# First convolution with band 8 mixed as well, squares issued ahead of casts, and the last projection one band later

## Chip, core and metric

One NeuronCore of a Trainium2 chip runs the whole program in one launch. The metric is device time in microseconds (us), the median of three runs. PE is the matrix engine (TensorE), DVE the vector engine, ACT the scalar engine, POOL GpSimd, SP the engine that here only issues DMAs.

## What is computed

The input x has shape (4, 128, 64, 64): batch, channels, rows, columns. Layer 0 is a group norm, four-head attention over all 4096 positions of an image, a projection and a residual sum. Layer 1 is the part that the change touches:

```python
residual = x
out = conv3x3_decomposed(x, lsq_quantize(w1, alpha1))
out = jax.nn.relu(batchnorm(out, gamma1, beta1))
out = conv3x3_decomposed(out, lsq_quantize(w2, alpha2))
out = batchnorm(out, gamma2, beta2)
out = jax.nn.relu(out + residual)
```

Both convolutions are 3x3 with 128 channels in and out and zero padding. All of it is float32; to keep that accuracy each convolution input is split into a high and a low part, and the products of both parts are summed in PSUM.

## The kernel before

Attention takes the first 2230 us or so and writes its result y0 to HBM. It works in 32 blocks of 512 positions; the last block's end (merge of its row sums, sums, reciprocal, weighing, projection, store) is left over and done within the first convolution.

The convolutions work in 16 bands, four for each image, of 16 rows each. A band's input tile t has 18 rows of 66 columns (a border of one on each side). The function `layer(i, prepare, start)` runs one convolution (i = 0 or 1). `BY_TWO[i]` says which bands go the mixed way:

- A **plain** band (`split_parts`, from line 594, and `conv`, line 813) casts t to a high part on ACT (L599, hi) and subtracts on DVE (L602, lo). PE then does 2 halves x 2 parts x 9 taps = 36 matmuls of 512 columns. The results' statistics are taken on DVE (L928) and the results copied to cv by ACT (L933).
- A **mixed** band (`mixed_parts`, line 570) makes sums and differences of rows first, so that two rows of output share products: DVE computes vo and vi (L580, L582, L583; "mix"), ACT casts them to uo and ui (L585), DVE subtracts to get lo and li (L589; "rest"). PE then does 4 results x 2 parts x 3 taps = 24 matmuls (`conv_by_two`, L846), the inner results from ui and li first, then the outer ones from uo and lo. From PSUM, ACT copies one inner result (L860, "copy"), DVE forms the inner sum and difference (L863, L865, "inner"), ACT writes the two outer results to a tile co (L870), and POOL adds co to cv by an accumulating DMA (L872). For the bands 13 and 14 DVE adds the outer results itself instead (L876, `outer_at_once`). The band's sum of squares is a pass of ACT over cv (L973, "square"), so it has to wait for that DMA.

Before the change bands 0, 1, 8 and 15 are plain in both convolutions, the others mixed.

The order of the work on each engine is written out by hand: each engine runs its instructions in the order in which the loop of `layer` emits them. At band m the loop emits: PE's matmuls of band m; then what the drain of band m and the preparation of band m + 2 need, that is ACT's copy, then `begin` (mix for band m + 2 on DVE and its casts on ACT), then `flush(1)` (the square of the mixed band before the last, kept in the list `behind`), then DVE's inner sums, `rest` for band m + 2, `later` (other work, and the load of band m + 3 by SP, with memsets of its border on POOL), and the outer results.

In the first convolution `first(m)` gives begin, rest and later. At band 3 its `begin` also weighs the last block's attention (L522), and its `later` holds the last block's projection (PE, L317) and store (a sum on DVE, L532, and a DMA on POOL, L533), then closes the attention's pools. The second convolution uses `second(m)`, whose `later` makes the next band's t by a ReLU on ACT (L1101) and loads the residual (L1138, SP). Eight of these residual loads also need nothing from the first convolution's results: SP issues them as soon as its queue comes to them, near the end of the first convolution.

The tiles t, hi, lo, vo, vi and co come from one ring of nine slots (`stack_tile`). PSUM has three double banks (tag s) and two single banks (tag a). A mixed band takes a double bank for the inner results, and for the outer ones either a second double bank or both single banks, alternating (`banks`); the projection and the last band (c_last) use single banks too.

```python
plain = [m for m in range(len(bandlist) - 1) if m not in BY_TWO[i]]
two = [m for m in range(len(bandlist) - 1) if m in BY_TWO[i]]
...
if (len(two) - 1 - two.index(m)) % 2:
    c = [psa.tile([P, FB], F32, name=f"c{i}_{b}_{g}{j}", tag="a") for j in "xy"]
else:
    c = pss.tile([P, 2, FB], F32, name=f"c{i}_{b}_{g}z", tag="s")
```

Of the kernel before, what the change touches and what calls it, by code (L numbers as in the profile page):

```python
# [78 lines left out]
def _fast_body(ctx, tc, x, norm_w, norm_b, qkv_wt, qkv_b, proj_wt, proj_b,  # L79
# [147 lines left out]
    def f32(t):  # L227
        return t.bitcast(F32)
# [336 lines left out]

    BY_TWO = (set(range(2, 15)) - {8}, set(range(2, 15)) - {8})

    def mixed_parts(t, name):  # L570

# [42 lines left out]
    def parts_of(i, m, t):  # L614
        b, g = bandlist[m]
        way = mixed_parts if m in BY_TWO[i] else split_parts
        mix, rest, ready[i, b, g] = way(t, f"{i}_{b}_{g}")
        return mix, rest
# [187 lines left out]
    def conv(parts, ps, j, w):  # L806
        hi, lo = parts
        r0 = j * RB
        n = 0
        for part in (hi, lo):  # L810
            for tap in range(TAPS):
                kh, kw = divmod(tap, 3)
                nc.tensor.matmul(ps.rearrange("p (r w) -> p r w", w=W), w[:, tap, :],  # L813
                                 part[:, r0 + kh : r0 + kh + RB, kw : kw + W],
                                 start=(n == 0), stop=(n == 2 * TAPS - 1))
                n += 1

    def conv_tile(i, b, g):
        return pss.tile([P, 2, FB], F32, name=f"c{i}_{b}_{g}", tag="s")
# [19 lines left out]
    def conv_by_two(parts, a, c, i):  # L839

        for m, ps, w in ((1, a[0], wmix[:, 0, :, :]), (2, a[1], wmix[:, 1, :, :]),
                         (0, c[0], wq[i][:, 0:3, :]), (3, c[1], wmix[:, 2, :, :])):
            n = 0
            for part in parts:
                for kw in range(3):
                    nc.tensor.matmul(ps.rearrange("p (r w) -> p r w", w=W), w[:, kw, :],  # L846
                                     part[m][:, :, kw : kw + W], start=(n == 0), stop=(n == 5))
                    n += 1
# [57 lines left out]
    def layer(i, prepare, start=None):  # L906


        plain = [m for m in range(len(bandlist) - 1) if m not in BY_TWO[i]]
        two = [m for m in range(len(bandlist) - 1) if m in BY_TWO[i]]  # L910
        st = mid.tile([P, 2 * len(plain), 6], F32, name=f"st{i}")
        sums = mid.tile([P, 4 * len(two)], F32, name=f"sums{i}")
        squares = mid.tile([P, len(two)], F32, name=f"squares{i}")
        shift = mid.tile([P, 2], F32, name=f"shift{i}")
        end = mid.tile([P, 18], F32, name=f"end{i}")
        n_plain, n_two = (float(len(u) * 2 * FB) for u in (plain, two))
        nc.gpsimd.memset(end[:, 0:1], n_plain)
        nc.gpsimd.memset(sums, 0.0)
        nc.gpsimd.memset(end[:, 3:4], n_two)

        behind = []

        def flush(left=0):
            while len(behind) > left:
                behind.pop(0)()

        def stats(m, j, ps):
            nc.vector.bn_stats(st[:, 2 * plain.index(m) + j, :], ps[:, j, :])  # L928

        def keep(m, j, ps):  # L930
            b, g = bandlist[m]
            c = 2 * g + j
            nc.scalar.copy(cv[b][:, c * FB : (c + 1) * FB], ps[:, j, :])  # L933

        def origin():
            mv = small.tile([P, 2], F32, name=f"first{i}", tag="mv")
            nc.vector.bn_aggr(mv, st[:, 0:2, :].rearrange("p j s -> p (j s)"))
            nc.vector.tensor_copy(shift[:, 0:1], mv[:, 0:1])
            nc.vector.tensor_scalar(shift[:, 1:2], mv[:, 0:1], -1.0, None, ALU.mult)

        def banks(m):
            b, g = bandlist[m]
            a = conv_tile(i, b, g)
# [4 lines that stand above are left out]
                c = [c[:, j, :] for j in range(2)]  # L948
            return [a[:, j, :] for j in range(2)], c

        done = start(banks, stats, keep, origin) if start else {}
        for m, (b, g) in enumerate(bandlist[:-1]):
            if m in done and m not in BY_TWO[i]:
                continue
            begin, rest, later = prepare(m)
            if m in BY_TWO[i]:
                if m in done:
                    a, c = done[m]
                else:
                    a, c = banks(m)  # L960
                    conv_by_two(ready[i, b, g], a, c, i)
                y = cv[b][:, 2 * g * FB : (2 * g + 2) * FB]
                k = two.index(m)
                copy, inner, outer, junk = rows_of_two(a, c, y, sums[:, 4 * k : 4 * k + 4], f"{i}_{m}",
                                                       m > 12)
                copy()
                begin()
                flush(1)
                inner()
                rest()  # L970
                later()
                outer()
                behind.append(lambda y=y, k=k, junk=junk: nc.scalar.activation(  # L973
                    junk, y, AF.Square, bias=shift[:, 1:2], accum_out=squares[:, k : k + 1]))
                continue
            ps = conv_tile(i, b, g)
            for j in range(2):
                conv(ready[i, b, g], ps[:, j, :], j, wq[i])
            begin()
            flush(1)  # L980
            rest()
            later()
            for j in range(2):
                stats(m, j, ps)
                keep(m, j, ps)
            if m == 0:
                origin()
        flush()
        nc.vector.bn_aggr(end[:, 1:3], st.rearrange("p j s -> p (j s)"))
        nc.vector.tensor_scalar(end[:, 2:3], end[:, 2:3], n_plain, None, ALU.mult)  # L990
        nc.vector.tensor_reduce(end[:, 4:5], sums, AX.X, ALU.add)
        nc.vector.tensor_reduce(end[:, 5:6], squares, AX.X, ALU.add)
        nc.vector.tensor_scalar(end[:, 4:5], end[:, 4:5], 1.0 / n_two, None, ALU.mult)
        off = small.tile([P, 1], F32, name=f"off{i}", tag="rs")
        nc.vector.tensor_tensor(off, end[:, 4:5], shift[:, 0:1], ALU.subtract)
        nc.vector.tensor_tensor(off, off, off, ALU.mult)
        nc.vector.scalar_tensor_tensor(end[:, 5:6], off, -n_two, end[:, 5:6], ALU.mult, ALU.add)
        b, g = bandlist[-1]
        for j in range(2):
            ps = psa.tile([P, FB], F32, name=f"c{i}_last{j}", tag="a")  # L1000
            conv(ready[i, b, g], ps, j, wq[i])
            c = 2 * g + j
            nc.vector.bn_stats(end[:, 6 + 6 * j : 12 + 6 * j], ps)
            nc.scalar.copy(cv[b][:, c * FB : (c + 1) * FB], ps)
        for f in prepare(len(bandlist) - 1):
            f()
        if i == 0:
            pools["bad"] = psa.tile([P, FB], F32, name="nbad", tag="a")
            nc.tensor.matmul(pools["bad"][0:1, 0:1], pools["big"], ones[:, 0:1], start=True, stop=True)
        keep_warm(10)  # L1010
        return batch_norm(i, end)
# [14 lines left out]
    def first(m):  # L1026
        begin = rest = nothing
        last = parts[len(blocks) - 1]
        if 2 < m < len(bandlist) - 2:
            begin, rest = parts_of(0, m + 2, raw[bandlist[m + 2]])  # L1030
        if m == 3:
            mix = begin

            def begin():
                last["weigh"]()
                mix()

        def later():
            if m == 3:
                last["project"]()  # L1040
                last["store"]()
                att.close()
                pools["low"] = ctx.enter_context(tc.tile_pool(name="low", bufs=1, reuse_waits="tile"))
                cv.extend(pools["low"].tile([P, N], F32, name=f"cv{b}") for b in (2, 3))
            if m == 5:
                nc.sync.dma_start(out=f32(wq[1]), in_=wqd)
            if m == 11:
                scales()
            if m == 14:
                count_bad()  # L1050
            if 2 < m < len(bandlist) - 3:
                load_band(*bandlist[m + 3])

        return begin, rest, later
# [571 lines left out]
```

## Time and profile before

| what | us |
|---|---|
| median of 3 runs | 2473.88 (2472.6 to 2473.94) |
| the profiled execution | 2472.39 |
| its span, first to last instruction | 2470.7 |
| PE busy | 2437.0 (99% of the span) |
| DVE busy | 2198.8 (89%) |
| ACT busy | 2179.9 (88%) |
| POOL busy | 300.1 (12%) |

The first convolution's bands stand from about 2234 to 2333 us in the span, the second's from 2337 to 2440; the output pass follows. Times in timelines are us from the span's start. A row of a timeline reads: start, duration, engine, line of the kernel, operation, what it writes <- what it reads, shape, count, and in brackets how long the engine sat idle before it and what ended that. A row of the chain reads: start, duration, engine and tile or line, count.

### The profile page before, as it was taken

What the parts mean: (1) busy time and instruction counts of PE and PEld (TensorE: products, weight loads), DVE (VectorE), ACT (ScalarE), POOL (GpSimd) and SP (SyncE); (2) the same over time, 40 slices, a digit from 0 to 9 for tenths busy, and PEclk for the clock granted to TensorE, in tenths of its full rate; (3) what the DMA queues carried; (4) which work ended last, traced back from release to release, by engine and by line L of the source; (5) the groups of instructions that cost most, each with busy time, mean ns of one, the idle gap of its engine ahead of it and who ended that gap; (6) DMA issues with size and microseconds to landing.
All of it is one profiled execution on the core that took longest, in us unless ns stands there. A gap on an engine that the chain in (4) does not pass through costs nothing.

```text
span 2470.7 us, 65042 instructions
## 1 busy us (share of the span) xinstructions
PE 2437.0 (99%) x28420; PEld 1449.8 (59%) x28420; DVE 2198.8 (89%) x1556; ACT 2179.9 (88%) x2436; POOL 300.1 (12%) x486
## 2 busy tenths in 40 slices
PE   9999999999999999999999999999999999999995
PEld 6555555555555555555555555555555555557774
DVE  6899888989998888899989888889999999999797
ACT  5999888999988899999998899999999999995687
POOL 2111111111011111111101111111010101011010
PEclk9999999999999999999999999999999999999997
DMA  6877677678776766688767676678666666778627
GB/s 197 189 187 167 174 176 176 167 192 207 167 163 168 181 161 165 144 206 200 174 155 174 172 174 155 158 190 205 147 145 142 152 138 142 161 150 163 154 52 239
DMA packets 154451, 415.67 MB, mean 168 GB/s; under 512 B 61968, under 2 KB 62736, under 8 KB 125488
## 3 DMA queue, kind: packets, MB, share of 16 engines
q0 software_dynamic: 48864, 291.93, 52.3%
q1 hardware_dynamic: 104576, 118.08, 17.6%
q8 instruction: 225, 3.69, 0.6%
q10 hardware_dynamic: 720, 1.44, 0.2%
q14 instruction: 66, 0.54, 0.1%
HBM read 107.75 MB, written 56.43 MB: 66 GB/s over the span
## 4 chain that ended last, share of the span: by engine, by line
PE 96%; DMA 1%; DVE 1%; issue 1%; ACT 0%; ACTq 0%; POOL 0%; SPq 0%; POOLq 0%; DVEq 0%
PE s L442 43%; PE acc L456 39%; PE c L846 3%; PE c L813 2%; PE l L488 1%; PE pq L317 1%; PE po L317 1%; PE pk L317 1%; PE pv L317 1%; DMA rm<-p 1%; PE c_last L813 1%; DVE res L1164 1%; PE c_3z L846 0%; PE c_2z L846 0%; DMA xh<-in_x_dram 0%
## 5 line engine op out<-in xcount | busy, mean ns | idle before, releaser
L444 ACT ACTIVATE p<-s 128x1024 f32<-128x1024 f32 x2048 | 1951.2, 1032 | 194.7 <-PE s L442 151.6
L471 DVE TENSOR_TENSOR r<-r,p 128x2048 f32<-128x2048 f32 x768 | 1758.1, 2289 | 62.9 <-ACT p L444 12.0
L442 PE MATMUL s<-q,k 64*128 64x512 f32 x8192 | 1136.8, 409 | 0.5 <-ACT p L444 0.5
L456 PE MATMUL acc<-p,v 128*32 128x256 f32 x16384 | 1025.8, 383 | 0.0
L442 PEld LDWEIGHTS s<-q,k 64*128 64x128 f32 x8192 | 715.5, 184 | 406.9 <-issue 164.2
L456 PEld LDWEIGHTS acc<-p,v 128*32 128x32 f32 x16384 | 462.7, 109 | 483.3 <-issue 247.8
L466 POOL DMA_DIRECT2D rm<-p x160 | 139.3, 871 | 774.2 <-ACT p L444 618.2
L352 DVE SCALAR_TENSOR_TENSOR kst<-pk,b,kst 128x512 fp32r<-128x512 f32 x32 | 24.0, 750 | 82.8 <-PE s L442 62.3
L469 DVE TENSOR_TENSOR r<-p,p 128x2048 f32<-128x2048 f32 x32 | 73.2, 2287 | 10.9 <-ACT p L444 10.9
L352 DVE SCALAR_TENSOR_TENSOR qst<-pq,b,qst 128x512 fp32r<-128x512 f32 x32 | 24.0, 751 | 59.0 <-PE s L442 48.0
L356 POOL DMA_DIRECT2D qd<-qst x31 | 23.1, 744 | 270.5 <-DVE qst L352 227.0
L492 POOL DMA_DIRECT2D r<-rm x32 | 27.0, 845 | 224.7 <-DMA rm<-p 72.0
L585 ACT CAST uo<-vo 128x1056 fp32r<-128x1056 f32 x24 | 25.9, 1080 | 22.0 <-DVE vo L580 21.7
L846 PE MATMUL c<-ui,wmix 128*128 128x512 f32 x144 | 42.2, 401 | 0.0
L846 PE MATMUL c<-li,wmix 128*128 128x512 f32 x144 | 42.0, 400 | 0.0
L356 POOL DMA_DIRECT2D kd<-kst x27 | 20.0, 742 | 177.0 <-DVE kst L352 168.3
L464 POOL DMA_DIRECT2D rm<-p x32 | 17.9, 559 | 172.6 <-ACT p L444 104.5
L351 ACT ACTIVATE kst<-pk,b 128x512 fp32r<-128x512 f32 x32 | 22.3, 700 | 17.9 <-PE pk L317 17.8
L488 PE MATMUL l<-r,ones 128*32 128x256 f32 x512 | 37.7, 379 | 0.0
L973 ACT ACTIVATE co<-cv,shift 128x1024 f32<-128x1024 f32 x24 | 27.5, 1148 | 10.1 <-DMA cv<-co 10.1
L533 POOL DMA_DIRECT2D y<-x x32 | 21.2, 663 | 124.9 <-DVE x L532 124.9
L317 PE MATMUL po<-av,wp 128*32 128x512 f32 x256 | 33.4, 593 | 0.4 <-DVE av L522 0.4
(270 smaller groups left out, 1213.1 us busy)
## 6 DMA issues: line engine op xcount, KB each, us to landing
rm<-p POOLq DMA_DIRECT2D x192, 1024.0 KB, 7.7
r<-rm POOLq DMA_DIRECT2D x32, 1024.0 KB, 7.6
q<-qd SPq DMA_DIRECT2D x248, 128.0 KB, 4.9
x<-in_x_dram SPq DMA_DIRECT2D x86, 256.0 KB, 5.6
k<-kd SPq DMA_DIRECT2D x124, 128.0 KB, 4.7
qd<-qst POOLq DMA_DIRECT2D x31, 512.0 KB, 4.8
kd<-kst POOLq DMA_DIRECT2D x27, 512.0 KB, 4.3
cv<-co POOLq DMA_DIRECT2D x20, 512.0 KB, 5.2
```

Of the source, the lines that this page charges most:

```text
L317: nc.tensor.matmul(out[cs, :], w[:, cs], x, start=True, stop=True)
L352: nc.vector.scalar_tensor_tensor(lo, ps[what], bias, t[:, 0, :], ALU.add, ALU.subtract)
L356: (nc.sync if start else nc.gpsimd).dma_start(out=dst[b, j].rearrange("s p n -> p s n"), in_=t)
L442: nc.tensor.matmul(s[:, i, :], k[r, half, c0 : c0 + P], q[r, half, part, :], start=(part == 0), stop=(part == 1))
L444: nc.scalar.activation(pts[step][:, 2 * half : 2 * half + 2, :], s, AF.Exp, scale=SCALE)
L456: nc.tensor.matmul(acc[n][h * D : (h + 1) * D, cs], v[:, kt % KB, h * D : (h + 1) * D], pt[:, h, cs], start=(kt == 0 and half == 0), stop= ...
L466: nc.gpsimd.dma_start(out=msum[n], in_=pt, accum_op=ALU.add)
L469: nc.vector.tensor_tensor(rsum[n], pts[step - 1], pt, ALU.add)
L471: nc.vector.tensor_tensor(rsum[n], rsum[n], pt, ALU.add)
L488: nc.tensor.matmul(t["l"][h * D : (h + 1) * D, cs], ones, r[:, h, cs], start=first, stop=end)
L813: nc.tensor.matmul(ps.rearrange("p (r w) -> p r w", w=W), w[:, tap, :], part[:, r0 + kh : r0 + kh + RB, kw : kw + W], start=(n == 0), stop ...
L846: nc.tensor.matmul(ps.rearrange("p (r w) -> p r w", w=W), w[:, kw, :], part[m][:, :, kw : kw + W], start=(n == 0), stop=(n == 5))
```

## The change

Three edits. Band 8 of the first convolution goes the mixed way too (the second convolution keeps it plain). In the branch of mixed bands, in both convolutions, `flush(1)` stands ahead of `begin()`, so that ACT's queue has the square of an earlier band ahead of the casts for band m + 2. The last attention block's projection and store, and the closing of the attention's pools, stand at band 4 of the first convolution instead of band 3.

```diff
-    BY_TWO = (set(range(2, 15)) - {8}, set(range(2, 15)) - {8})
+    BY_TWO = set(range(2, 15)), set(range(2, 15)) - {8}
...
                 copy()
+                flush(1)
                 begin()
-                flush(1)
                 inner()
                 rest()
                 later()
...
         def later():
-            if m == 3:
+            if m == 4:
                 last["project"]()
                 last["store"]()
                 att.close()
```

As a result the first convolution has 13 mixed bands instead of 12, and `two.index(m)` of bands 9 to 14 grows by one, so the alternation of PSUM banks keeps its place for bands 9 to 14 and is turned over for bands 2 to 7.

## The prediction, made before the changed kernel had run

> **What bounds the kernel now.** First the page's chain of work that ended last: it is TensorE (PE) for 96% of the span, and PE is busy for 99%. So an edit counts by what it does to PE's own work, or by making PE wait. The change touches the two convolution stages only (2234 to 2440 us), so I then asked for busy time by stretch: bands 2 to 7, plain band 8, bands 9 to 14 of the first convolution.
>
> ```profile
> core 0: us, PE busy (x) PEld busy (x) DVE busy (x) ACT busy (x) POOL busy (x), PEclk, DMA share, GB/s
> 2245.90:2281.50 35.60, 35.60 (x153) 27.16 (x152) 33.36 (x52) 25.32 (x46) 5.80 (x18) 1.00 0.98 188
> 2281.50:2290.10 8.60, 8.60 (x37) 6.78 (x37) 5.63 (x8) 3.91 (x8) 1.29 (x7) 1.00 1.18 233
> 2290.10:2324.40 34.30, 34.30 (x145) 27.08 (x144) 32.48 (x57) 24.78 (x44) 4.00 (x11) 1.00 0.83 199
> ```
>
> PE has no gap at full clock, but VectorE (DVE) is 94 and 95% busy beside the mixed bands. Only plain band 8 gives it air: 5.63 of 8.60 us. Next the chain in order of time (start, duration) gives PE's price per band: 36 matmuls of a plain band 8.58 us; the first 12 of a mixed band's 24 2.87, so 5.72 a band.
>
> ```profile
> 2281.70 8.58 PE c L813 x36
> 2290.29 2.87 PE c L846 x12
> ```
>
> DVE's timeline shows one whole mixed loop: mix (L580 to L583), inner sums (L863, L865), rest (L589), then the next mix.
>
> ```profile
> 2299.84 1.25 DVE L580 TENSOR_TENSOR vo<-t 128x1056 f32<-128x1056 f32 x1
> ...
> 2303.58 1.25 DVE L589 TENSOR_TENSOR lo<-vo,uo 128x1056 fp32r<-128x1056 f32 x1
> 2304.75 1.25 DVE L589 TENSOR_TENSOR li<-vi,ui 128x1056 fp32r<-128x1056 f32 x1
> 2305.92 1.25 DVE L580 TENSOR_TENSOR vo<-t 128x1056 f32<-128x1056 f32 x1
> ```
>
> From mix to mix 6.08 us: DVE needs 0.36 us more than PE per mixed band, and lives on a lead. The lead is read where PE takes li, its second operand of a band. Band 14's li is written at 2317.59 + 1.25 = 2318.84; PE reads it at:
>
> ```profile
> 2319.42 0.88 PE L846 MATMUL c<-li,wmix 128*128 128x512 f32 x3
> ```
>
> 0.58 us are left at the end of the stage. This is what the change spends.
>
> [...] The rows above have 1.25 (1.17 from start to start). [...] I go by the trace's 6.08. [...] the accumulating transfer that a square waits for (cv<-co, POOL's queue) lands in 5.3 us alone, but in 9.8 and 8.9 beside the residual loads (L1138, SP's queue). I go by those:
>
> ```profile
> DMA to landing us min/median/max: 5.3/8.9/9.8
> ```
>
> **The change part by part.**
>
> *Band 8 mixed, PE.* 12 matmuls fewer: 8.58 - 5.72 = **-2.86 us**, the most that the whole change can give (0.12%).
>
> *Band 8 mixed, DVE.* Out: one lo (1.31 from start to start) and two statistics (about 1.3); in: mix 2.41, inner sums 1.34, rest 2.34. That is +3.5 us in a stage shorter by 2.86. Out too is DVE's wait of 2.96 for a stack slot that plain band 8 held. I carry DVE's queue on from its mix for band 7 (2268.81, unmoved, see below), 6.08 a loop. Mix for band 8 stands at 2274.89, and li of a band is done 6.16 after its mix. PE's read of li without waits is the trace's for bands 2 to 8, then each 5.72 later:
>
> - band 8: done 2281.05, PE 2282.26; band 9: 2287.13, 2287.98; band 10: 2293.21, 2293.70; band 11: 2299.29, 2299.42;
> - band 12: 2305.37, 2305.14: PE late by 0.23; band 13: 2311.45, 2310.86: 0.59 in all;
> - band 14: DVE also does the six scale products (0.66) first: 2318.19, 2316.58: 1.61 in all.
>
> PE's late start doesn't delay DVE in turn (its next inputs from PE are ready a microsecond ahead). So **+1.61 us** of waits for li, where there was none.
>
> *Band 8, the rest.* ACT gets two casts, copy, two outer rows and a square for one cast and two copies, about +2.9 us; it is 3.91 of 8.60 busy there. POOL issues one more cv<-co (0.85, 512 KB). Both hide behind PE and DVE. The bank parity flips for bands 2 to 7: same waits, one band apart.
>
> *Squares ahead of casts* (25 after the change). A square takes 1.15 us, 1.25 with its read. ACT waits for vo before most casts (14.1 us in 9 waits in the first convolution), and the square falls into that. DVE takes uo 3.74 after its mix, while the cast ends 2.42 after it: 1.3 us of room. So nothing, if the square's transfer has landed. ACT reaches it 6.3 us after the transfer's issue (two loops, 12.16, less the casts, outer rows and copies between). It is free while landing takes under about 7.4: then square 1.15, casts 2.06, outer rows 1.15 and the 0.35 to the issue fill two loops. Landings in mid-stage are 5.2 to 7.0. From 0 to the rival's price below; I take 0. In the second convolution likewise, as the loop is the same 6.08.
>
> *Band 13.* Here the square is band 11's, and its transfer lands beside the residual loads. Before, the cast of plain band 15 was ahead of it; now it is behind:
>
> ```profile
> 2318.93 1.19 ACT L599 CAST hi<-t 128x1188 fp32r<-128x1188 f32 x1
> 2321.96 1.15 ACT L973 ACTIVATE co<-cv,shift 128x1024 f32<-128x1024 f32 x1 [1.84 <-DMA cv<-co]
> ```
>
> Queued behind: cast hi (1.19), on DVE lo (1.39), then the first outer sum (0.68), which frees the PSUM bank for c_last. With hand-overs 4.44 us from landing to c_last. The issue was 2312.11; with the square of band 9 out of the way and DVE 0.7 ahead I get 2310.3. Landing after 8.9 to 9.8: 2319.2 to 2320.1, so c_last starts at 2323.6 to 2324.5. By li it could start at 2324.43 - 2.86 + 1.61 = 2323.18. **+0.45 to +1.35, taken 0.9.** In the second convolution c_last starts at 2431.39, so landing must be by 2426.95. The issue (2420.88) comes some 2.1 earlier and ahead of two of the four loads that stood before it; even at the trace's 8.3 it lands at about 2427. Taken 0; unmoved at 2429.22 it would cost 2.3.
>
> *Projection and store a band later.* PE 0.99 us either way. The store sum (0.74) and DVE's wait behind it move from ahead of band 6's mix to ahead of band 7's:
>
> ```profile
> 2261.93 0.58 POOL L533 DMA_DIRECT2D y<-x  x1 [6.28 <-DVE x L532]
> ...
> 2262.72 1.26 DVE L580 TENSOR_TENSOR vo<-t 128x1056 f32<-128x1056 f32 x1 [1.10 <-POOL t L546]
> ```
>
> POOL issues the store, then the memsets of the next band's border, for which DVE's mix waits 1.10. Both are in the 2268.81 above. Band 3's cv<-co, held on POOL till 2262.59 though ACT was done by 2259.6, goes earlier; band 4's is held instead. SP's queue gets no new wait: the stored rows are loaded for band 15, 40 us later. The projection's bank is freed 0.7 us before band 5 needs it (1.26 before). Nothing.
>
> **Sum:** -2.86 + 1.61 + 0.9 + 0 = **-0.35 us**. The profiled execution took 2472.39 (span 2470.7 and 1.7 around it), so 2472.0 by it; it stands 1.5 below the median of the three runs, and carried to that, 2473.88 - 0.35 = **2473.5**. About 0.2% (5 us) is what a measurement of this kernel tells from no change.
>
> **Rivals.**
> - *DVE keeps up* (14%). If the waits for li or the bank don't come, -1.6 to -2.86: 2471.0 to 2472.3. For it: DVE's 2.96 wait is gone. Against it: 6.08 against 5.72 holds in every loop of the trace.
> - *The residual loads hold the squares longer* (22%). Loads start about 2 us earlier too; a landing 1 us later costs 1 us in the first convolution, and up to 2.3 in the second: 2474.6 to 2476.8.
> - *Slower: the squares' landings set ACT's pace* (6%). Place: square ahead of cast, in every mixed band. From 7.4 us of landing on, two bands take landing + 4.7 instead of 12.16. At 8.9 for bands 4 to 12 that is 0.73 x 9 = 6.6, less 1.2 of lead: +5.4, so 2478.9. For it: 8.9 is the median late in the stage. Against it: the earlier transfers land in 5.2 to 7.0.
>
> **Chances.** The forecast's case (2472.6 to 2474.5) has 58%. For 8 times in 10: part of the first rival and nearly all of the second, 2471.6 to 2476.3. Faster by over 0.2%: 2% (more than -2.86 has no source); slower: 6%; within: 92%.
>
> **What would show it.** No plain band 8 (24 matmuls at L846, -2.86). PE idle before li at L846 in bands 12 to 14, released by DVE, about 1.6 us in all. c_last held by an L876 sum behind a square that waited for DMA at band 13. The 1.10 wait for POOL's memset one band later. No waits of casts on squares elsewhere. The second convolution's length unchanged. Wrong if li waits are absent, if landings in mid-stage pass 7.4, or if the second convolution moves by over 1 us.

## The result, and the profile after

| | before | after |
|---|---|---|
| median of 22 runs each, us | 2472.88 (2471.35 to 2474.9) | 2476.39 (2474.71 to 2479.43) |
| the profiled execution, us | 2472.39 | 2476.46 |
| its span, us | 2470.7 | 2474.7 |

The ratio is 1.0014, with a 95% interval of 1.0008 to 1.0020: 3.5 us slower, where 2473.5 (2471.6 to 2476.3) had been forecast.

A total of 2475 us hides where it went, so I cut each trace at seven points: TensorE's first mixed matmul of band 2; the start of c_last in the first convolution and the end of the statistics on it (`bn_stats`); TensorE's first matmul of the second convolution; the start of c_last and the end of the statistics there; and the end of the last work of VectorE and ACT. What attention did before the first point (here 0.4 us less than before) and the landing of the last store (7.45 us before, 7.27 after) fall out.

| stretch, us | before | after | difference |
|---|---|---|---|
| first convolution, band 2 to the start of c_last | 78.53 | 79.29 | +0.76 |
| c_last to the end of the statistics | 9.51 | 9.59 | +0.08 |
| between the convolutions | 2.92 | 2.93 | 0.00 |
| second convolution, start to the start of c_last | 94.53 | 96.74 | +2.21 |
| c_last to the end of the statistics | 9.50 | 11.08 | +1.58 |
| output pass | 22.35 | 22.35 | 0.00 |

So +0.84 comes from the first convolution, where -0.35 was forecast, and +3.79 from the second, where the forecast had zero. Both come out in the busy time by stretch (the columns are those of the view shown in the prediction; the stretches are bands 2 to 7, band 8, bands 9 to 14, and then three stretches of 3.41 us around c_last of the second convolution):

```profile
core 0: us, PE busy (x) PEld busy (x) DVE busy (x) ACT busy (x) POOL busy (x), PEclk, DMA share, GB/s
2245.51:2281.15 35.64, 35.64 (x154) 27.05 (x152) 32.93 (x50) 24.87 (x45) 5.59 (x18) 1.00 0.95 188
2281.15:2286.88 5.73, 5.73 (x26) 4.52 (x25) 5.70 (x10) 4.59 (x10) 0.68 (x4) 1.00 1.12 179
2286.88:2323.99 37.11, 36.01 (x145) 26.39 (x143) 34.17 (x58) 27.28 (x49) 5.75 (x19) 1.00 1.11 228
2431.53:2434.94 3.41, 1.41 (x7) 0.84 (x6) 3.03 (x6) 1.81 (x3) 0.00 (x0) 1.00 1.00 299
2434.94:2438.35 3.41, 3.41 (x10) 2.62 (x9) 2.58 (x11) 2.64 (x6) 0.00 (x0) 0.50 0.35 135
2438.35:2441.76 3.41, 3.41 (x16) 2.69 (x15) 1.40 (x6) 0.59 (x2) 0.00 (x0) 1.00 0.02 5
```

Band 8 takes 5.73 us in place of 8.60: the 2.86 are there. Bands 9 to 14 take 37.11 in place of 34.30: 2.81 us of it given back. Only 1.10 us of the 2.81 show as idle time of TensorE in this view. The starts in TensorE's timeline show them all: from band 9 on the bands start 5.88, 6.06, 6.10, 6.07 and 6.08 us apart, before the change 5.71 to 5.73. And in the second convolution there is something that no view of before had shown within the convolutions: after a stretch in which TensorE was busy for 1.41 of 3.41 us, it got half its clock (PEclk 0.50) for the next 3.41 us.

TensorE's timeline of the changed kernel has the waits themselves: the last li of the first convolution, and c_last of both:

```profile
2318.70 0.99 PE L846 MATMUL c<-li,wmix 128*128 128x512 f32 x3 [0.75 <-DVE li L589]
...
2324.80 2.38 PE L813 MATMUL c_last<-hi,wq 128*128 128x512 f32 x9 [0.81 <-DVE cv L876]
...
2434.05 3.47 PE L813 MATMUL c_last<-hi,wq 128*128 128x512 f32 x9 [2.00 <-DVE cv L876]
2437.32 2.78 PE L813 MATMUL c_last<-lo,wq 128*128 128x512 f32 x9
2439.93 2.33 PE L813 MATMUL c_last<-hi,wq 128*128 128x512 f32 x9
```

Both waits for the bank end with the sum at L876. The second one is 2.00 us, and behind it nine matmuls take 3.47 and 2.78 us before they are back at 2.33. Before the change, c_last of the second convolution had neither wait nor half clock:

```profile
2431.39 2.31 PE L813 MATMUL c_last<-hi,wq 128*128 128x512 f32 x9
```

ACT's timeline names what L876 itself was waiting for: band 11's square, which now stands ahead of the cast of band 15. First the second convolution of before, then that of the changed kernel:

```profile
2426.99 1.19 ACT L599 CAST hi<-t 128x1188 fp32r<-128x1188 f32 x1
2429.24 1.15 ACT L973 ACTIVATE co<-cv,shift 128x1024 f32<-128x1024 f32 x1 [1.06 <-DMA cv<-co]
```

```profile
2429.55 1.16 ACT L973 ACTIVATE co<-cv,shift 128x1024 f32<-128x1024 f32 x1 [4.28 <-DMA cv<-co]
2430.61 0.19 ACT L973 ACTIVATION_READ_ACCUMULATOR co<-cv,shift 128x1 f32 x1
2430.70 1.17 ACT L599 CAST hi<-t 128x1188 fp32r<-128x1188 f32 x1
```

In the changed kernel ACT stood for 4.28 us until band 11's transfer had landed, and only behind the square could it do the cast. VectorE's lo needs that cast (VectorE was idle for 5.18 us ahead of it), and the sum at L876 stands behind lo in VectorE's queue. This is the chain that the prediction described for band 13. It had put its cost at 0.9 us in the first convolution (0.81 came) and at nothing in the second.

### The profile page after: what moved, and what is told of

Its sections match the earlier page's. It is cut to its first block, busy times and chain, and to the rows that moved or that the text cites. A ratio compares the mean times of both kernels' runs of the same rounds, so it can differ in the third digit from the quotient of the medians.

```text
span 2474.7 us, 65036 instructions
## 1 busy us (share of the span) xinstructions
PE 2437.7 (99%) x28408; PEld 1448.0 (59%) x28408; DVE 2202.0 (89%) x1562; ACT 2184.6 (88%) x2442; POOL 301.0 (12%) x487
## 4 chain that ended last, share of the span: by engine, by line
PE 93%; DVE 3%; issue 1%; DMA 1%; ACT 1%; ACTq 0%; POOL 0%; POOLq 0%; DVEq 0%
PE s L442 44%; PE acc L456 39%; PE c L813 1%; PE l L488 1%; PE pq L317 1%; DMA cv<-co 1%; PE po L317 1%; PE pv L317 1%; PE pk L317 1%; PE c_last L813 1%; DVE res L1164 1%; PE idle L310 1%; PE c L846 1%; DVE vo L580 0%; DVE lo L589 0%
## 5 line engine op out<-in xcount | busy, mean ns | idle before, releaser
L846 PEld LDWEIGHTS c<-li,wmix 128*128 128x128 f32 x150 | 27.7, 188 | 10.7 <-DVE li L589 3.7
```

## The experiments

Stage differences below are from the traces, against the trace of before, cut as above. Each run's median is given with that of the runs of the kernel before on the same chip.

**One part alone: the order.**

```diff
 (kernel before)
                 copy()
+                flush(1)
                 begin()
-                flush(1)
```

> The kernel before with one edit: in mixed bands the square is issued ahead of the casts (band 8 of the first convolution stays plain, projection and store stay at band 3). My theory: the loss comes from band 13, where the square of band 11 stands ahead of the cast of band 15 and waits for its transfer among the residual loads; c_last starts 4.6 us after that landing. First convolution: landing at 2320.5 to 2321.5, so c_last at 2325.1 to 2326.1 against 2324.43 before: +0.7 to +1.7 us. Second: the hold on GpSimd's issue belongs to the last transfer here, so band 11's is issued 1.2 us earlier than in the changed kernel, lands at 2427.4 to 2428.2 and costs 0 to 0.8 us, without a fall of the granted clock. Sum +0.7 to +2.4, about +1.5 us against before. Rival (the loss comes from the mixed band 8 and its overloaded VectorE): 0. Rival (squares set ACT's pace in every band): +3 or more, with waits of TensorE in mid-stage.

Measured: 2472.82 against 2472.87, ratio 1.0001 (0.9993 to 1.0009). First convolution +0.66, nearly all of it c_last's wait for the bank (0.44 shows as idle time); second convolution 0.00. Band 11's transfer there was issued at 2419.11 and landed at 2426.22; the square waited 0.99 us for it, and c_last not at all. The mechanism is as expected. The sum by the trace (+0.66) is just under the expected range, and the medians show no change. The order alone doesn't make the second convolution longer.

**The rest alone: band 8 and the projection.**

```diff
 (changed kernel)
                 copy()
-                flush(1)
                 begin()
+                flush(1)
```

> The changed kernel with the square behind the casts again, so band 8 mixed and the projection and store at band 4 (they belong together: at band 3 the projection would ask for a bank that holds that band's own outer results, which are read after it). My theory: -2.86 of matmuls, +1.6 of waits for li in the last bands, no wait of c_last, second convolution unchanged: -1.25 us against before (between -0.4 and -1.6). GpSimd's issue is held 1.2 us at band 11's transfer of the second convolution as in the changed kernel, but nobody on the path waits for it. Rival (band 8 or the moved projection makes the loss): +1 to +3.5 against before.

Measured: 2472.55 against 2472.87, ratio 0.9998 (0.9990 to 1.0006). First convolution -0.95, that is -2.86 and +1.9 of waits for li, which begin at band 11; second convolution -0.02. So neither part makes the loss: it needs both.

**Band 13 alone put back.**

```diff
 (changed kernel)
                 copy()
+                if m == 13:
+                    begin()
                 flush(1)
-                begin()
+                if m != 13:
+                    begin()
```

> The changed kernel, but at band 13 alone, in both convolutions, the square goes behind begin() again. My theory: c_last's two waits (0.8 and 2.0 us) go, and with the second one the half clock (3.4 us at 0.5, worth 1.7 us) that followed it: -3.5 to -4.5 us against the changed kernel, -0.4 (0 to -0.8) against before. Rival (the half clock has another cause, such as the moment or the load): it stays, and only 2.8 us go. Rival (the squares of the other bands or band 8 make the loss): within 1 us of the changed kernel.

Measured: 2472.6 against 2472.87, ratio 1.0000 (0.9991 to 1.0008). Both waits for the bank are gone, the mean granted clock on record is 0.995 in all 13 runs (0.994 in the traced execution of the changed kernel), first convolution -0.20, second +0.04. Band 13's square is the whole of the second convolution's loss, half clock included. The difference to the run before, 0.75 us in the first convolution, is what the other bands' squares cost there.

**The bank.** c_last in a double bank, with the order of the changed kernel. The first form changes the bank alone; the second also puts both halves' matmuls ahead of the statistics and copies. Of its edit only the lines of the bank are shown.

```diff
 ...
-            ps = psa.tile([P, FB], F32, name=f"c{i}_last{j}", tag="a")
+        both = conv_tile(i, b, g)
 ...
```

> The changed kernel with the order of all instructions kept, but c_last in a double bank (tag s; the slot that band 13's inner results leave) in place of the single banks that band 13's outer results hold until the sum at L876. My theory: the square of band 11 still waits 3 to 4 us for its transfer, but the cast of band 15 ends at about the time when TensorE finishes band 14, so c_last starts without the bank wait: 2323.99 in the first convolution and 2432.05 in the second (by the changed kernel's clock), no half clock; -0.4 us (0 to -0.8) against before. Rival (c_last really waits for the late cast or for lo of band 15, not for the bank): it still starts 1 to 2 us late.

> The changed kernel with c_last in a double bank, as in the run last_in_pss, but now with both halves' matmuls ahead of the statistics and copies of the first half; in that run the second half waited 4.6 and 4.0 us for the copy of the first, since both halves lie in one tile. Its first half had started with no wait in the first convolution and 0.24 us late in the second, for the cast. My theory: c_last starts with waits of 0 and 0.2 us, no half clock; -3.5 us against the changed kernel, -0.4 (0 to -0.8) against before. Rival (the bank isn't what delays c_last): within 1 us of the changed kernel.

Measured: first form 2485.0 (ratio 1.0047, 1.0034 to 1.0061), second form 2476.2 (1.0014, 1.0008 to 1.0021). What they were made for they show: c_last's first half starts with no wait in three of the four convolutions, and 0.24 us late, for the cast, in the fourth. So the bank was what held c_last. The gain that I had expected isn't there, because other waits came with the move. In the first form the second half waited 4.61 and 3.96 us for ACT's copy of the first, which lies in the same tile. In the second form:

```profile
2331.03 2.32 PE L813 MATMUL c<-lo,wq 128*128 128x512 f32 x9
2333.40 2.50 PE L310 MATMUL idle<-gavg 128*128 128x128 f32 x20
2338.13 3.08 PE L813 MATMUL c<-hi,wq 128*128 128x512 f32 x9 [2.23 <-POOL sums L918]
```

The idle matmuls between the convolutions (`keep_warm`, 20 in the row) waited 1.29 us for ACT's copy of c_last in the changed kernel, since they use a single bank too, and so filled part of the pause. With c_last elsewhere they ran at once, TensorE then stood still for 2.23 us, and the first nine matmuls of the second convolution took 3.08 us (2.39 in the changed kernel). From c_last to the end of the statistics it is 1.3 us longer than before in each convolution: the first half's statistics now wait until TensorE is done with both halves (2.39 us of idle time of VectorE in the second convolution), and the second half's for ACT's copy of the first (0.65 us). This is a confirmed cause and a failed remedy.

**The landing.** The last eight residual loads in the other order, so that SP's first load waits for a tile that comes free late and is issued at 2424.49.

```diff
-    for b in (B - 2, B - 1):
+    for b in (B - 1, B - 2):
```

> The changed kernel with the last eight residual loads of the second convolution in the other order (batch 3 ahead of batch 2), so that SP first waits for slots that come free only behind band 14 and none of the eight loads runs beside band 11's transfer. My theory: that transfer, still issued at about 2420.3, lands in 4.5 to 5.7 us as in mid-stage, by 2426, so c_last has no wait and there is no half clock: the second convolution is 3.7 us shorter. What the late loads cost the output pass I can't tell from a trace: 8 x 512 KB at some 200 GB/s are 21 us, which end about 2455 to 2460 in place of 2440 to 2445, for 0 to +10 us in the pass. Rival (the landing of 9.2 us has another cause than the loads): it still lands 8 to 9 us after its issue.

Measured: 2473.45 against 2472.66, ratio 1.0006 (0.9997 to 1.0014). The DMA view of one microsecond around the issue of band 11's transfer (last column: us to landing), in the changed kernel and in this one:

```profile
cv<-co POOLq DMA_DIRECT2D x1, 512.0 KB, 9.2
```

```profile
cv<-co POOLq DMA_DIRECT2D x1, 512.0 KB, 4.5
```

The same transfer, in the same place, landed in 4.5 us without the loads of SP's queue beside it, and in 9.2 with them. c_last doesn't wait, the clock doesn't fall (nine matmuls of c_last take 2.30 to 2.33 us), the second convolution is at +0.03, and the output pass is 22.35 us as before: the late loads cost nothing. The 200 GB/s of the expectation is an estimate near what the stretches of before had shown, 188 to 233.

**The issue.** GpSimd's timeline in the second convolution, of the kernel before and of the changed one. A row's bracket is GpSimd's idle time ahead of the issue:

```profile
2420.88 0.86 POOL L872 DMA_DIRECT2D cv<-co  x1 [5.04 <-ACT co L870]
2428.18 0.86 POOL L872 DMA_DIRECT2D cv<-co  x1 [6.19 <-ACT hi L599]
```

```profile
2412.99 0.86 POOL L872 DMA_DIRECT2D cv<-co  x1 [5.10 <-ACT co L870]
2420.32 0.86 POOL L872 DMA_DIRECT2D cv<-co  x1 [6.28 <-issue]
```

Set beside the end of the outer rows on ACT, the issue follows 0.30 us later for nearly every band; but at 2428.18 (band 12, before) and at 2420.32 (band 11, after) it follows 1.55 us later, with nothing on record that it waits for. "issue" in the bracket of the second says just that; the bracket of the first names a cast that the transfer doesn't read. In both programs it is the 381st DMA that GpSimd issues; in the changed kernel the mixed band 8 has added one ahead of it. So I took one away, at the other end of the program:

```diff
-    bp = column(proj_b, "bp")
+    bp = const.tile([P, 1], F32, name="bp")
+    nc.sync.dma_start(out=bp, in_=proj_b.rearrange("(c o) -> c o", o=1))
```

> The changed kernel, with one tiny load of the very start (proj_b, 0.5 KB) issued by SP in place of GpSimd, so that GpSimd issues one DMA less in the whole program. In all six traces so far GpSimd's DMA number 381 is issued 1.55 us after the outer rows are done, against 0.30 for its neighbours; with the mixed band 8 that number is band 11's transfer of the second convolution. My theory: here number 381 is band 12's again, band 11's is issued at about 2419.1 instead of 2420.3, lands 7.1 to 8.3 us later, at 2426.2 to 2427.4; c_last (landing + 4.6) then starts with no wait to 0.7 us of wait after band 14's end at 2432.05, and the clock doesn't fall. Gain against the changed kernel 3 to 3.8 us: about 2472.7, -0.2 against before (-0.8 to +0.8). Rival (the hold belongs to the moment or to the instruction, not to the count): band 11's transfer is still held, and the time stays at 2476.4.

Measured: 2473.95 against 2472.66, ratio 1.0005 (0.9997 to 1.0014). The hold has moved to the next transfer, band 12's, as GpSimd's timeline shows:

```profile
2419.93 0.85 POOL L873 DMA_DIRECT2D cv<-co  x1 [5.04 <-ACT co L871]
2427.22 0.86 POOL L873 DMA_DIRECT2D cv<-co  x1 [6.18 <-issue]
```

Band 11's lands 7.2 us after its issue, c_last doesn't wait, its matmuls keep to 2.30 to 2.32 us for nine, and the second convolution is at +0.03. A 0.5 KB load issued by another engine 2.4 ms earlier takes away 3.8 us of the trace. The median fell by 2.4; the first convolution keeps its +1.07.

**The clock.** Unused matmuls between band 14 and c_last in the second convolution, first 14, then 8.

```diff
+        if i == 1:
+            warm = pss.tile([P, 2, FB], F32, name="warm", tag="s")
+            for _ in range(14):
+                nc.tensor.matmul(warm[:, 0, 0:P], gavg, gavg, start=True, stop=True)
```

> The changed kernel with 14 small matmuls (128 columns, results unused, in a free double bank) between band 14 and c_last in the second convolution: they run in the 2.0 us in which TensorE waits for the bank, 0.125 us each, 1.75 us in all. My theory: the wait itself stays (c_last starts about 2434, 2 us late), but TensorE isn't idle, so the granted clock stays at 1.0 and c_last takes 8.6 us in place of 10.4: 1.7 us less than the changed kernel, 2474.7. Rival (the half clock doesn't come from the idle time): 3.4 us at 0.5 as in the changed kernel, and no gain.

> As the run filler, with 8 unused matmuls in place of 14. In that run each became two passes of 0.109 us, so the 14 took 3.04 us and held c_last until 2435.80, 1.04 us longer than the bank did; the granted clock stayed at 1.0 and c_last took 8.7 us. Eight take 1.74 us, less than the wait of 2.0. My theory: c_last starts when the bank is free, as in the changed kernel, the clock stays at 1.0, and the second convolution is 1.5 to 1.7 us shorter than in the changed kernel's trace; the median of the times falls by less if not every execution of the changed kernel had the half clock. Rival (0.3 us of idle time and more suffice for the half clock): it comes back.

Measured: 2476.52 (ratio 1.0015, 1.0008 to 1.0022) and 2476.25 (1.0013, 1.0007 to 1.0020). The 14 were mis-sized: the rows of `keep_warm` give 0.125 us each (2.50 us for 20), but a row counts every one of these matmuls twice (28 for the 14), so they ended after the bank came free. With 8, TensorE's timeline and two stretches of its clock read:

```profile
2433.10 1.95 PE L1002 MATMUL warm<-gavg 128*128 128x128 f32 x16
2435.50 2.39 PE L813 MATMUL c_last<-hi,wq 128*128 128x512 f32 x9 [0.45 <-DVE cv L876]
```

```profile
2433.20:2436.60 3.40, 2.95 (x22) 2.57 (x21) 3.22 (x7) 2.05 (x5) 0.00 (x0) 1.00 0.93 278
2436.60:2440.00 3.40, 3.40 (x16) 2.69 (x15) 2.57 (x11) 2.17 (x4) 0.00 (x0) 1.00 0.34 123
```

c_last is as late as in the changed kernel, but at full clock: c_last to the end of the statistics is 9.58 us in place of 11.08. With 0.45 us of idle time ahead of c_last in place of 2.00 the clock stayed at 1.00: so here the half clock came from TensorE's idle time. The median, though, is within 0.2 us of the changed kernel's, so the half clock is probably not in most of that kernel's executions: without it the trace's difference is 4.63 - 1.5 = 3.1 us, near the 3.5 of the medians. In 7 of the changed kernel's 22 runs the mean clock on record is under 0.995, in none of the 39 runs with unused matmuls; and the median of those 7 is 0.9 us above that of the other 15. That points the same way and doesn't prove it, since only one execution was traced.

**A version from the findings.** Squares behind the casts, band 8 mixed, and two moves that give VectorE back its lead.

```diff
 (run no_order)
         def later():
+            if 2 < m < len(bandlist) - 3:
+                load_band(*bandlist[m + 3])
             if m == 4:
                 last["project"]()
...
-            if m == 11:
-                scales()
             if m == 14:
+                scales()
                 count_bad()
-            if 2 < m < len(bandlist) - 3:
-                load_band(*bandlist[m + 3])
```

> The run no_order (band 8 mixed, projection and store at band 4, squares behind the casts), with two moves that give VectorE back its lead in the first convolution: the load of band 7 and its memsets on GpSimd stand ahead of the projection and the store at band 4 (VectorE's mix for band 7 waited 1.16 us for them behind the store), and the six scale products (0.66 us) go from band 11 to band 14, where VectorE prepares no further band. My theory: in no_order TensorE waited 1.9 us for li in bands 11 to 14; with 1.8 us of lead more, nearly all of it goes. First convolution -2.5 to -2.8 us against before, second unchanged: about 2470.2. Rival (li isn't what holds TensorE there, or the moves make other waits): -1.0 as in no_order.

Measured: 2470.82 (2469.58 to 2472.84) against 2472.71, ratio 0.9993 (0.9985 to 1.0001). Its three stretches of the first convolution, bands 2 to 7, 8, and 9 to 14:

```profile
2246.67:2282.30 35.63, 35.63 (x154) 27.16 (x153) 34.75 (x52) 24.78 (x45) 5.86 (x18) 1.00 0.99 194
2282.30:2288.00 5.70, 5.70 (x26) 4.49 (x25) 5.67 (x10) 4.54 (x10) 1.09 (x4) 1.00 1.07 182
2288.00:2322.39 34.39, 34.39 (x146) 27.03 (x144) 32.89 (x53) 26.43 (x47) 5.07 (x15) 1.00 1.06 225
```

TensorE is busy all through: the first convolution is 2.80 us shorter than before, all but 0.06 of what band 8 can give, and the second is unchanged. By the medians the gain is 1.9 us; the interval just reaches no change.

## Why the prediction failed, step by step

- **Band 8's matmuls, -2.86.** Right.
- **Waits for li, +1.61.** Mis-sized: 2.81. The mechanism was right, and in the kernel without the new order the size was nearly right too (1.9). The forecast let VectorE's mix for band 7 stand "unmoved" at 2268.81 and put the squares' order at nothing, as "landings in mid-stage are 5.2 to 7.0" (4.5 to 7.0 by the trace of before). But the first transfer of the stage, band 2's, takes longer, 7.8 us before and 8.2 after, above the 7.4 that the prediction had set as the limit, and I had left it out of "mid-stage". ACT, VectorE and VectorE again, at bands 4 and 5 of the changed kernel:

```profile
2262.74 1.15 ACT L973 ACTIVATE co<-cv,shift 128x1024 f32<-128x1024 f32 x1 [2.12 <-DMA cv<-co]
```

```profile
2264.99 1.26 DVE L589 TENSOR_TENSOR lo<-vo,uo 128x1056 fp32r<-128x1056 f32 x1 [0.67 <-ACT uo L585]
2269.25 1.26 DVE L580 TENSOR_TENSOR vo<-t 128x1056 f32<-128x1056 f32 x1 [1.17 <-POOL t L551]
```

  Band 2's square waited 2.12 us, the cast behind it was late, and VectorE lost 0.67 us of lead. Its wait for the memsets behind the store moved by a band as forecast (1.17 for 1.10). Counted from the first mixed matmul, the mix for band 7 stands 0.83 us later than before, in the kernel without the new order 0.06. From then on each of VectorE's loops of 6.08 us comes that much later for TensorE, which waits from band 9 on in place of band 12. No run put band 2's square back alone.
- **Band 13 in the first convolution, +0.9.** Right: 0.81 of wait; band 11's transfer was issued at 2310.79 (2310.3 forecast) and landed after 9.4 us.
- **The second convolution, "taken 0".** This step failed. It rested on an issue of band 11's transfer "some 2.1 earlier". Counted from the start of the convolution it came 1.0 earlier, since the mixed band 8 of the *first* convolution had pushed GpSimd's hold of 1.25 us onto just this transfer; in the two runs in which another transfer has the hold (the order alone, and one DMA less) it came 2.3 earlier. And it landed after 9.2 us, not 8.3, still among the loads. So the landing moved by only 0.2 us, and the price that the prediction gave for an unmoved landing, 2.3, is about what the wait cost (2.21). The rival that the residual loads hold the squares longer named this place, and its range, which ended at 2476.8, has the measured time in it; the hold on the issue it did not have. The sign of being wrong that the prediction had named for this, a second convolution that moves by over 1 us, came true.
- **The half clock, no term at all.** It added 1.5 us in the traced execution, and less in the median.
- **Projection and store, 0.** Right as far as a trace can tell: the wait of VectorE behind the store moved along with them, and I found no other. They were not tried without band 8.

The two experiments on one part each show what the sum left out: by the traces +0.66 and -0.95 add up to -0.3, near the -0.35 forecast, while both together make +4.6. The 4.9 us between are an interaction. In the second convolution, with 3.8 of them, the order makes c_last depend on band 11's landing, band 8 delays the issue of that transfer, and the loads stretch it; taking away any one of the three takes away all of the 3.8. The other 1.1 stand in the first convolution, where VectorE has less lead than before and the squares take more of it; they stay when the loads or the one DMA are moved.

## What to carry to other kernels

In the changed kernel a square that stood 4.28 us for its transfer passed its wait on to what stood behind it in ACT's queue, and 2.00 us of it came to TensorE. Before moving such an instruction ahead, price it with the slowest landing of its transfer in the whole trace (9.8 us before the change), not with the usual one (5.2, the median), and follow what is queued behind to the last consumer. Parts of a change that are each worth nothing can meet in one place: here one DMA more on GpSimd put an issue 1.25 us late on the very transfer that the new order had made TensorE wait for. So look in the trace at when every later transfer is issued. And where one engine feeds another with a lead of under a microsecond (0.58 us here, at the end of the stage), look first for moves that give it more lead (here two, worth 1.8 us by the traces), before adding work.

## What the runs showed of the hardware

- **TensorE's clock fell behind 2 us of idle time.** In the changed kernel's trace the granted clock is 0.50 from 2434.94 to 2438.35, and again from 2448.59, three times 3.41 us after the rise; in the trace of before it falls once, at 2444.86. I cut both traces into stretches of 3.413 us, counted from these falls. Those just ahead of a fall hold 2.00 and 1.97 us of idle time of TensorE (changed kernel) and 2.48 (before). All others in which it partly worked hold at most 1.29 (changed kernel, from 2332.54) and 1.22 (before, from 2332.24), and have full clock behind them; what lies between 1.29 and 1.97 these two traces don't show. The fall at c_last cost 1.5 us in the traced execution; half of 3.41, 1.7 us, is my estimate of the most that one such stretch can cost.
- **The 381st DMA that GpSimd issues left 1.25 us late** in the traces of the kernel before, of the changed kernel and of the run with one DMA less: 1.55 us after the outer rows were done, in place of 0.30, though it is band 12's transfer in the first and the third and band 11's in the second. Its place among GpSimd's instructions doesn't explain it: it is the 805th, the 806th and the 810th of them, and with one DMA less the 805th, band 11's transfer, went without a hold. The 188th and the 278th were late too, before and after the change: 1.41 us behind the end of VectorE's instruction that makes what they send. With one DMA less the transfer that was the 188th is the 187th, and the one behind it has the wait with nothing on record (0.79 us). Both in the kernel before, and with one DMA less:

```profile
1051.08 0.75 POOL L356 DMA_DIRECT2D qd<-qst  x1 [12.47 <-issue]
1051.82 0.90 POOL L466 DMA_DIRECT2D rm<-p  x1
```

```profile
1050.28 0.75 POOL L357 DMA_DIRECT2D qd<-qst  x1 [11.35 <-DVE qst L353]
1051.82 0.85 POOL L467 DMA_DIRECT2D rm<-p  x1 [0.79 <-issue]
```

  The 140th left 1.07 us behind the end of its VectorE instruction (772.63 in the trace of before). Whether that one goes by the count, and what happens at these places, no run tells.
- **A 512 KB accumulating transfer**, band 11's in the second convolution, landed in 4.5 us without the residual loads beside it (the run with the loads in the other order), in 7.1 and 7.2 when issued a little ahead of most of them (the runs with the order alone and with one DMA less), and in 9.2 in their midst (the changed kernel).
